# A two-layer graph attention kernel: the order of the setup, and where the first panel's q takes its operands from

## Chip, core and metric

The kernel runs on one core of one Trainium2 chip. The metric is the device time of one execution in microseconds (us); lower is better. The engines are named as the profile names them: PE (TensorE; PEld is its weight load), DVE (VectorE), ACT (ScalarE), POOL (GpSimd) and SP (SyncE). All matrix work is in float32.

## What is computed

Two graph attention layers over N = 2708 nodes with D = 1024 features, each after a layer norm and relu, each added to its input:

```
# layer 0
h = maximum(layernorm(x), 0)
f = h @ Wf + bf;  g = h @ Wg + bg
e = relu(f @ g.T)
scores = where(adj > 0, e, -9e15)
x = x + softmax(scores, axis=1) @ (h @ W + bW)
# layer 1
h = maximum(layernorm(x), 0);  h2 = h @ W1
e = leaky_relu(h2 @ a1 + (h2 @ a2).T, 0.2)
x = x + relu(softmax(where(adj > 0, e, -9e15), axis=1) @ h2)
```

adj is an int32 matrix of N x N with mostly zeros.

## The kernel before

**Layer 0 without f and g.** The kernel forms M = Wf Wg' once (1024 x 1024), so that the scores of all rows against the panel p of columns are h (M h_p') plus bias terms: `project_q(p)` computes q = M' h' for a panel (called B), `scores(p)` multiplies the transposed rows of h with it. The bias terms are dot products on DVE: u and v (weights with bf and bg), r (rows with v).

**Tiling.** The 2708 rows are 22 tiles, 20 of 128 rows and two of 74; they are treated in 11 pairs q = 0..10, the two short tiles being pair 2. The columns are five panels of 586, 586, 512, 512 and 512. Every large product is one level of Strassen and Winograd: seven products of half size named M1, M5, M6, M7, M3, M2, M4, whose operands are sums and differences of blocks, so both the left and the right sides exist in seven variants.

**Setup.** wg's and wf's row chunks (128 x 1024) are loaded and transposed on PE (`transposed_wg` L367, `transposed_wf` L378; PSUM tiles wT_ps), copied to SBUF by DVE and ACT in turn (`copy`, L156), and multiplied: M is made in 16 half rows of eight 128x512 matmuls (`half_row_of_M`, L389, tile M_ps). The half rows with a = 0..7 and b = 0 come first, then those with b = 1. `left_of_q(k)` forms the sums of M's blocks. All 28 left sides (7 products x 4 blocks of 128x512) are written by POOL to the DRAM tensor md_d (`store_M`, L383).

**Rows.** For each pair: `fetch` loads x in four halves; `norms` does the layer norm (DVE statistics, ACT square root L237, ACT relu L249); `rows` is `pair_h`, which forms four sums of halves with `add` and `sub` on DVE into g1 and g2 and writes five pieces to hg_d on POOL (L262 to L264; the right sides of the aggregation later); `dots` gives r; `transposes` transposes the four halves on PE (L299, tile h_ps) and copies them out on ACT (L300, hsT); `sums` forms the four remaining left sides of the scores and writes eight blocks of 128x512 to hs_d[q] on POOL (L312, L313; short pair L316, L317). hsT is a pair of large tiles from a pool (`both`, gts) with a single buffer each; project_q's transposed rows hT are allocated from the same two.

**The order.** These steps stand in a list `later`, each with a cost in us. Between products the program calls `behind(us)`, which adds credit and issues list items until it is used up; `make_until(q)` issues whatever is left up to a pair. The list of before is: for pairs 0 to 3 (EARLY) everything; for pairs 4 to 8 (AHEAD 5) norms, rows, dots; then, for each pair from 4 on, transposes and sums, and norms to dots of the pair five later. Credit is given from half row a = 4 on, 6.5 us per half row. An item that takes PSUM banks is issued only where banks are free, which `scores(0)` gives through make_until(q + 2).

**project_q(0).** It loads the panel's transposed rows (ten loads of hT from hs_d, lo and hi, L121 through `load`), forms T1 (tile qT1) from them, and for each of the seven products loads the left sides (two loads of md from md_d, 0.5 MB each into stream tiles). The products are issued in `accumulate` (L444; PSUM tiles qx, qy, qz) in the order M1, M2, M5, M6, M3, M7, M4; x, y and z are groups of four banks. Evictions go to ACT (M1, M2: m1, B) and DVE (the others).

**scores(p).** For each pair q: make_until(q + 2), the adjacency load of pair q + 2, and products (L877; PSUM sx, sy, sz) in the order M1, M6, M5, M2, M7, M3, M4. Every second product loads its two left sides from hs_d into a stream tile As. M4 of a pair is issued after M1 of the next. The mask of pair q + 1 is converted on DVE after M5, and its transposes on PE with ACT's copies and POOL's write to mk_d (`turn`, L574 to L581) come before M3.

**Queues and buffers.** All loads (`load`, L121) are issued by SP in program order; a load that waits for its buffer holds the loads behind it. The tile framework places instructions and semaphores; in scores of layer 0 the order on DVE is held as written. There are 54 slots (2.3 KB per partition), 12 stream tiles (4 KB per partition) and 8 PSUM banks. g1, g2, md and As are stream tiles; x halves, M and masks are slots.

Of the kernel before, what the change touches and what calls it, by code (L numbers as in the profile page):

```python
# [18 lines left out]
P = 128  # L19
# [37 lines left out]
def kernel(  # L57
# [103 lines left out]
    def put(us, go, fetch=None, takes_psum=False):  # L161
        later.append([us, fetch, go, takes_psum])

    def one():
        for it in later[:2]:
            if it[1]:
                it[1]()
                it[1] = None
        us, _, go, _ = later.pop(0)
        go()  # L170
        return us

    def behind(us, psum_free=False):
        credit[0] = min(credit[0] + us, 2 * us)
        while later and credit[0] > 0 and (psum_free or not later[0][3]):
            credit[0] -= one()
# [5 lines left out]
    def row_to_all(v, name):  # L182
        t = stream(name)
        load(t, bass.AP(tensor=v.tensor, offset=v.offset, ap=[[0, P], [1, D]]))
        return t
# [65 lines left out]
    def pair_h(l, q, ha, hb):  # L251

        n = rows_of[q]
        g1, g2 = stream("g1", (P, 2, W)), stream("g2", (P, 2, W))
        s1, s2, s3, s4 = g1[:n, 0], g1[:n, 1], g2[:n, 0], g2[:n, 1]
        add(s1, ha[1], hb[1])
        sub(s2, s1, ha[0])
        sub(s3, ha[0], ha[1])
        sub(s4, hb[0], s2)
        i, j = group_of[q]  # L260
        for m, h in ((M1, ha[0]), (M2, hb[0]), (M4, hb[1])):
            nc.gpsimd.dma_start(hg_d[l][i][:n, m, j], h)  # L262
        nc.gpsimd.dma_start(hg_d[l][i][:n, M5:M6 + 1, j], g1[:n])
        nc.gpsimd.dma_start(hg_d[l][i][:n, M7:M3 + 1, j], g2[:n])  # L264
# [6 lines left out]
    EARLY, AHEAD = 4, 5  # L271
    made = [0]

    def make_pairs():
        xs, hT = {}, {}

        def fetch(q):
            xs[q] = []
            for t in pairs[q]:
                r0, n = tiles[t]  # L280
                xs[q].append(row_halves("x", n))
                for e in range(2):
                    load(xs[q][-1][e], x[r0:r0 + n, e * W:(e + 1) * W])

        def norms(q):
            for k in range(2):
                normalize(xs[q][k])

        def rows(q):
            pair_h(0, q, *xs[q])  # L290

        def transposes(q):
            n = rows_of[q]
            lo, hi = (t[:, :4 * W].rearrange("p (m c j) -> p m c j", m=4, j=P) for t in both("hsT"))
            hT[q] = lo, hi
            for k, e, o in ((0, 0, lo[:, 0]), (0, 1, lo[:, 3]), (1, 0, hi[:, 3]), (1, 1, hi[:, 2])):
                ps = bank("h_ps", (P, NH, P))
                for c in range(NH):
                    nc.tensor.transpose(ps[:, c, :n], xs[q][k][e][:, c * P:(c + 1) * P], ident[:n, :n])  # L299
                nc.scalar.copy(o[:, :, :n], ps[:, :, :n])  # L300

        def sums(q):
            n = rows_of[q]
            lo, hi = hT.pop(q)
            i = lambda t, k: t[:, k, :, :n]
            add(i(lo, 2), i(hi, 3), i(hi, 2))
            sub(i(lo, 1), i(lo, 2), i(lo, 0))
            sub(i(hi, 0), i(lo, 0), i(hi, 3))
            sub(i(hi, 1), i(lo, 3), i(lo, 1))
            if n == P:  # L310
                flat = lambda t: t.rearrange("p m c j -> p (m c j)")
                nc.gpsimd.dma_start(flat(hs_d[q][:, 0:4]), flat(lo))  # L312
                nc.gpsimd.dma_start(flat(hs_d[q][:, 4:8]), flat(hi))  # L313
            else:
                rows = lambda t: t[:, :, :, :n].rearrange("p m c j -> p (m c) j")
                nc.gpsimd.dma_start(rows(hs_d[q][:, 0:4]), rows(lo))  # L316
                nc.gpsimd.dma_start(rows(hs_d[q][:, 4:8]), rows(hi))  # L317

        def dots(q):
            n = rows_of[q]  # L320
            for k, t in enumerate(pairs[q]):
                dot(r_[:n, t:t + 1], xs[q][k], [vb[e][:n, :W] for e in range(2)], c0[:n])

        def last(q):
            sums(q)
            xs.pop(q)
            made[0] = q + 1

        def start(q):
            put(4.2, lambda: norms(q), lambda: fetch(q))  # L330
            put(2.7, lambda: rows(q))
            put(3.2, lambda: dots(q))

        def end(q):
            put(0.5, lambda: transposes(q), takes_psum=True)
            put(2.7, lambda: last(q))

        for q in range(EARLY):
            start(q)
            end(q)  # L340
        for q in range(EARLY, EARLY + AHEAD):
            start(q)
        for q in range(EARLY, NQ):
            end(q)
            if q + AHEAD < NQ:
                start(q + AHEAD)
# [11 lines left out]
    bfb, bgb = row_to_all(bf, "bfb"), row_to_all(bg, "bgb")  # L358
    wgT, wfT, M = [None, None], {}, {}

    def transposed_wg(b):
        ws = [load_rows(wg, 4 * b + i, "wg") for i in range(4)]
        wgT[b] = [slot(f"wgT{c}_{b}")[:, :W] for c in range(NC)]
        for c in range(NC):
            ps = bank("wT_ps")
            for i in range(4):
                nc.tensor.transpose(ps[:, i * P:(i + 1) * P], ws[i][:, c * P:(c + 1) * P], ident)  # L367
            copy(wgT[b][c], ps)
        for i in range(4):
            dot(u[:, 4 * b + i:4 * b + i + 1], halves(ws[i]), halves(bfb))  # L370

    def transposed_wf(a):
        wt = load_rows(wf, a, "wf")
        wfT[a] = [slot(f"wfT{a}_{e}", (P, NH, P)) for e in range(2)]
        for e in range(2):
            ps = bank("wT_ps", (P, NH, P))
            for c in range(NH):
                nc.tensor.transpose(ps[:, c, :], wt[:, e * W + c * P:e * W + (c + 1) * P], ident)  # L378
            copy(wfT[a][e], ps)
        dot(v[:, a:a + 1], halves(wt), halves(bgb))  # L380

    def store_M(m, k, s):
        nc.gpsimd.dma_start(md_d[:, m, k, :], s)  # L383

    def half_row_of_M(a, b):

        ps = bank("M_ps")
        for c in range(NC):
            nc.tensor.matmul(ps, wfT[a][c // NH][:, c % NH, :], wgT[b][c], start=(c == 0), stop=(c == NC - 1))  # L389
        M[a, b] = slot(f"M{a}_{b}")[:, :W]  # L390
        copy(M[a, b], ps)
        if b == 0:
            store_M(M1 if a < NH else M2, a % NH, M[a, b])

    def left_of_q(k):
        a11, a12, a21, a22 = M.pop((k, 0)), M.pop((k + NH, 0)), M.pop((k, 1)), M.pop((k + NH, 1))
        s1, s2, s4 = (slot(f"ms{i}")[:, :W] for i in range(3))
        add(s1, a21, a22)
        store_M(M5, k, s1)
        sub(s2, s1, a11)  # L400
        store_M(M6, k, s2)
        sub(s4, a12, s2)
        store_M(M3, k, s4)
        sub(a21, a11, a21)
        store_M(M7, k, a21)
        store_M(M4, k, a22)

    make_pairs()
    transposed_wg(0)
    ahead = [0, 1, 2, 3, 4, 5, 6, 7]  # L410
    for a in range(NC):
        for _ in range(2):
            if ahead:
                transposed_wf(ahead.pop(0))
        half_row_of_M(a, 0)
        if a == NH:
            dot(c0, halves(bfb), halves(bgb))
            vb = [slot(f"vb{g}") for g in range(2)]
            for g in range(2):
                spread(vb[g][:, :W], [v[:, 4 * g + j:4 * g + j + 1] for j in range(4)])  # L420
            transposed_wg(1)
        if a >= NH:
            behind(6.5, True)
    for k in range(NH):
        for a in (k, k + NH):
            half_row_of_M(a, 1)
            wfT.pop(a)
            behind(6.5, True)
# [34 lines left out]
    def project_q(p, then={}):  # L463
# [3 lines left out]
        R = both("hT")  # L467
        lo, hi = (t.rearrange("p (c i) -> p c i", c=NH) for t in R)
        o = 0
        for t, (_, n) in enumerate(panels[p], first[p]):  # L470
            q, k = pair_of[t]
# [20 lines left out]
        def left(m, k, d):  # L492
            if m not in L:
                L[m] = [stream(f"md{m}", (P, 2, W)) for _ in range(2)]
                for g in range(2):
                    load(L[m][g], md_d[:, m, 2 * g:2 * g + 2, :])
            return L[m][k // 2][:, k % 2, d * P:(d + 1) * P]
# [8 lines left out]
        def sides(m):  # L506
            for g in range(2):
# [6 lines left out]
                else:  # L514
# [12 lines left out]
                   rate=2.0 if p == 0 else 1.5)  # L527
# [272 lines left out]
    wab = [consts.tile([P, D], FP, name=f"wab{k}") for k in range(2)]  # L800
# [6 lines left out]
    def prepare_W():  # L807
        ab, rows = [], {}

        def fetch(l, k):  # L810
            if l == 1 and not ab:
                for k2, a in enumerate((a1, a2)):
                    load(wab[k2], bass.AP(tensor=a.tensor, offset=a.offset, ap=[[0, P], [1, D]]))
# [37 lines left out]
    def scores(p, B):  # L851
# [50 lines left out]
        for q in range(NQ):  # L902
# [27 lines left out]
            if q + 1 < NQ:  # L930
                turn(q + 1)
            product(q, M3, Y, False)
            add(sa[:n, hi], Y[:n, :h], t[:n, lo])
            finish(q, sa, 0)
            behind(2 * rate, True)
# [5 lines left out]
    def softmax(p, S, m):  # L941
# [20 lines left out]
        later[:0] = [[1.4, None, (lambda i=i: go(i)), False] for i in range(len(order) + LAG)]  # L962
# [125 lines left out]
    def weights1(p, z, m):  # L1088
# [25 lines left out]
        for i in range(len(order) + LAG):  # L1114
            mk = []
            front.append([2.1, (lambda i=i, mk=mk: mk.append(load_mask(p, *order[i]))) if i < len(order) else None,
                          (lambda i=i, mk=mk: go(i, mk)), False])
# [65 lines left out]
```

## Time and profile before

| | |
|---|---|
| median of 3 runs | 3252.6 us (3251.47 to 3255.28) |
| profiled execution | 3251.27 us |
| its span | 3249.5 us |
| mean granted PE clock | 0.986 |
| first matmul of a half row of M | 17.34 us from the start |
| last half row of M ends | 143.4 us |
| first qx product (project_q(0)) | 158.78 us |
| first sx product (scores(0)) | 221.63 us |
| scores(0) ends | 412.94 us |

The page lists per engine the busy time, its share of the span and the number of instructions; then the same in 40 slices of equal length, each digit being tenths (9 is 90% or more), with the clock that TensorE was granted. A line of waits names the engine, what it wanted to do and its line, and after the arrow the engine or transfer and the tile that it waited for, with the total in us, the number of times and the longest. A timeline line has the start and the length in us, then the engine, line, operation, output tile, input tiles, number of instructions, and in brackets the idle time before it. "issue" is waiting that the profile could not put down to an event.

### The profile page before, as it was taken

The numbers are of one execution on the slowest core, as the hardware profiler recorded it, in microseconds if no ns is written. First come the engines' busy times: TensorE is split into PE (matmuls) and PEld (weight loads), VectorE is DVE, ScalarE is ACT, GpSimd is POOL, SyncE is SP. The second block draws the span as 40 slices with busy tenths as digits, with TensorE's granted clock in tenths as the row PEclk, the third lists the DMA queues.
The fourth block names the chain that finished last, engine by engine and source line by source line (L and its number), as shares of the span: only waits on it lengthen the run. The fifth ranks groups of instructions, "written<-read, shape, count | busy, mean of one in ns | idle before, by whom it ended". The sixth has DMA issues, their size and how long they took to land.

```text
span 3249.5 us, 35289 instructions
## 1 busy us (share of the span) xinstructions
PE 3136.1 (97%) x12924; PEld 2330.0 (72%) x12924; DVE 1753.1 (54%) x3648; ACT 499.9 (15%) x833; POOL 326.2 (10%) x410
## 2 busy tenths in 40 slices
PE   8898999999999999999999999996999999999999
PEld 5376777757877578885888885873766748778585
DVE  6856586275732676417672368637665282553712
ACT  2321120010200101101020002103221030221300
POOL 1411001210002110011000101021010000000001
PEclk9999999999999999999999999997999999999999
DMA  5987848565545576457654565765555445555646
GB/s 222 366 276 269 288 160 301 178 225 184 179 131 158 171 249 208 147 184 228 220 181 153 162 200 194 236 236 201 187 166 172 149 154 175 183 191 175 197 149 213
DMA packets 284012, 651.17 MB, mean 200 GB/s; under 512 B 51742, under 2 KB 121362, under 8 KB 281280
## 3 DMA queue, kind: packets, MB, share of 16 engines
q1 hardware_dynamic: 252480, 535.31, 51.1%
q0 software_dynamic: 31360, 113.62, 9.3%
q8 instruction: 102, 1.67, 0.2%
q14 instruction: 70, 0.57, 0.1%
HBM read 535.23 MB, written 113.58 MB: 200 GB/s over the span
## 4 chain that ended last, share of the span: by engine, by line
PE 77%; issue 6%; DVE 4%; DMA 3%; POOL 1%; ACT 1%; POOLq 0%; SPq 0%; DVEq 0%; ACTq 0%
PE gz L444 12%; PE gy L444 12%; PE gx L444 12%; PE sz L877 7%; PE sy L877 5%; PE gv L444 5%; PE sx L877 5%; PE pz L780 4%; PE py L780 3%; PE px L780 3%; PE qz L444 3%; PE qy L444 2%; PE qx L444 2%; DMA hs_d<-hsT 1%; PE mk_ps L574 1%
## 5 line engine op out<-in xcount | busy, mean ns | idle before, releaser
L877 PE MATMUL sz<-B,As 128*128 128x256 f32 (+3 forms) x1320 | 327.5, 397 | 2.9 <-DVE st L44 2.9
L877 PEld LDWEIGHTS sz<-B,As 128*128 128x128 f32 (+1 forms) x1320 | 247.6, 188 | 62.3 <-DVE st L44 3.8
L877 PE MATMUL sx<-B,As 128*128 128x256 f32 (+3 forms) x880 | 224.2, 398 | 13.0 <-DMA As<-hs_d 9.5
L877 PE MATMUL sy<-B,As 128*128 128x256 f32 (+3 forms) x880 | 222.3, 395 | 0.0
L444 PE MATMUL gx<-P,hc 128*128 128x256 f32 (+3 forms) x880 | 204.9, 395 | 4.7 <-ACT P L1107 4.7
L444 PE MATMUL gy<-T,hc 128*128 128x256 f32 (+3 forms) x880 | 205.8, 395 | 3.7 <-DMA hc<-hg_d 2.8
L444 PE MATMUL gz<-Sa,hc 128*128 128x256 f32 (+3 forms) x880 | 206.6, 393 | 0.0
L444 PE MATMUL gz<-P,hc 128*128 128x256 f32 (+3 forms) x880 | 206.3, 393 | 0.0
L877 PEld LDWEIGHTS sx<-B,As 128*128 128x128 f32 (+1 forms) x880 | 164.6, 188 | 53.2 <-issue 9.9
L715 POOL TENSOR_TENSOR gT<-gT,rr 128x2048 f32<-128x2048 f32 (+3 forms) x20 | 68.3, 3433 | 1324.8 <-DVE rr L44 704.2
L444 PEld LDWEIGHTS gx<-P,hc 128*128 128x128 f32 (+1 forms) x880 | 168.6, 192 | 41.1 <-ACT P L1107 5.0
L444 PEld LDWEIGHTS gy<-T,hc 128*128 128x128 f32 (+1 forms) x880 | 168.6, 192 | 39.5 <-DVE wT L44 3.3
L444 PEld LDWEIGHTS gz<-Sa,hc 128*128 128x128 f32 (+1 forms) x880 | 165.5, 190 | 31.9
L444 PEld LDWEIGHTS gz<-P,hc 128*128 128x128 f32 (+1 forms) x880 | 165.5, 190 | 31.9
L877 PEld LDWEIGHTS sy<-B,As 128*128 128x128 f32 (+1 forms) x880 | 160.7, 187 | 34.9 <-issue 0.7
L780 PE MATMUL px<-w,gT 128*128 128x512 f32 x320 | 145.1, 606 | 11.9 <-issue 10.4
L780 PE MATMUL py<-w,ps 128*128 128x512 f32 (+1 forms) x352 | 155.6, 592 | 0.3 <-DVE mcol L44 0.3
L780 PE MATMUL pz<-w,ps 128*128 128x512 f32 (+1 forms) x352 | 155.0, 592 | 0.0
L575 ACT COPY mask<-mk_ps 128x1024 bf16<-128x1024 bf16 (+1 forms) x55 | 55.7, 1013 | 563.8 <-PE mk_ps L574 263.0
L780 PEld LDWEIGHTS pz<-w,ps 128*128 128x128 f32 (+1 forms) x352 | 65.4, 186 | 85.6 <-issue 82.5
L780 PEld LDWEIGHTS py<-w,ps 128*128 128x128 f32 (+1 forms) x352 | 65.4, 186 | 85.6 <-issue 82.5
L780 PEld LDWEIGHTS px<-w,gT 128*128 128x128 f32 x320 | 61.7, 194 | 88.2 <-issue 84.0
(232 smaller groups left out, 4723.9 us busy)
## 6 DMA issues: line engine op xcount, KB each, us to landing
hc<-hg_d SPq DMA_DIRECT2D x350, 512.0 KB
As<-hs_d SPq DMA_DIRECT2D x150, 512.0 KB
w<-wt_d SPq DMA_DIRECT2D x96, 512.0 KB
w<-in_L_gnn_W_dram SPq DMA_DIRECT2D x72, 512.0 KB
md<-md_d SPq DMA_DIRECT2D x70, 512.0 KB
adj_i<-in_adj_dram SPq DMA_DIRECT2D x50, 512.0 KB
hg_d<-g POOLq DMA_DIRECT2D x40, 512.0 KB, 6.1
hs_d<-hsT POOLq DMA_DIRECT2D x20, 1024.0 KB, 8.2
```

What stands on the lines that cost most here:

```text
L444: nc.tensor.matmul(ps[d], left(m, k, d), right(m, k), start=(start and k == 0), stop=(k == K - 1), skip_group_check=True)
L574: nc.tensor.transpose(ps[:n, k, i * P:(i + 1) * P], m[0][:, i, k, :n], identb)
L575: nc.scalar.copy(mk[:n, :, :k4 * P], ps[:n, :, :k4 * P])
L715: nc.gpsimd.tensor_tensor(of(e, s), of(e, s), by(s, k), OP.mult)
L780: nc.tensor.matmul(ps, left[i][m][:, k, :], w_[k], start=(start and k == 0), stop=(k == NH - 1), skip_group_check=True)
L877: nc.tensor.matmul(ps[:n, :h], lefts[q][:, i % 2, c, :n], B[m][c // 2][:, c % 2, :h], start=(start and c == 0), stop=(c == NH - 1), skip_g ...
```

## The change

- wg's four chunks are loaded first, bf and bg after them and among wf's chunks; the two broadcasts live in their own tiles (wab, used later for a1 and a2).
- The first wg block is transposed chunk by chunk into eight banks; wf's, the second wg block's and M's copies out of PSUM are all on ACT; the dots of wg with bf are spread, one per half row.
- The list of due steps is reordered: norms(q + 1), rows(q), transposes(q), dots(q), sums(q), all pairs alike; credit is given from the first half row on (2.0, from a = 4 on 5.0, in the second half 5.5).
- pair_h's four sums are on POOL in layer 0 and stay on DVE in layer 1.
- hsT is four stream tiles, written to hs_d by four DMAs. Where a tile of the pair belongs to panel 0, DVE copies the transposed rows from PSUM also into first_h, the two hT tiles of project_q(0).
- The left sides stay in SBUF slots (m_left) and project_q(0) takes them there; md_d is still written for the other panels.
- project_q(0) gives 1.2 us of credit per product part in place of 2.0; in scores, in all panels, the mask's transposes come after M3 and finish.

```diff
     def pair_h(l, q, ha, hb):
+        on = nc.vector if l else nc.gpsimd
...
-        add(s1, ha[1], hb[1])
-        sub(s2, s1, ha[0])
-        sub(s3, ha[0], ha[1])
-        sub(s4, hb[0], s2)
+        on.tensor_tensor(s1, ha[1], hb[1], OP.add)
+        on.tensor_tensor(s2, s1, ha[0], OP.subtract)
+        on.tensor_tensor(s3, ha[0], ha[1], OP.subtract)
+        on.tensor_tensor(s4, hb[0], s2, OP.subtract)
...
         def transposes(q):
-            lo, hi = (t[:, :4 * W].rearrange("p (m c j) -> p m c j", m=4, j=P) for t in both("hsT"))
+            ts = [stream("hsT", (P, 2, NH, P)) for _ in range(4)]
...
-                nc.scalar.copy(o[:, :, :n], ps[:, :, :n])
+                nc.scalar.copy(hT[q][1](i), ps[:, :, :n])
+                t = pairs[q][k]
+                if panel_of[t] == 0:
+                    o = tiles[t][0]
+                    nc.vector.tensor_copy(first_h[e].rearrange("p (c i) -> p c i", c=NH)[:, :, o:o + n], ps[:, :, :n])
...
-        for q in range(EARLY):
-            start(q)
-            end(q)
-        for q in range(EARLY, EARLY + AHEAD):
-            start(q)
-        for q in range(EARLY, NQ):
-            end(q)
-            if q + AHEAD < NQ:
-                start(q + AHEAD)
+        put_norms = lambda q: put(4.2, lambda: norms(q), lambda: fetch(q))
+        put_rows = lambda q: put(0.5, lambda: rows(q))
+        put_dots = lambda q: put(3.2, lambda: bias(q), ready=lambda: vb[0] is not None)
+        put_norms(0)
+        for q in range(NQ):
+            if q + 1 < NQ:
+                put_norms(q + 1)
+            put_rows(q)
+            put(0.5, lambda q=q: transposes(q), takes_psum=True)
+            if q > 1:
+                put_dots(q)
+            put(2.7, lambda q=q: last(q))
+            if q == 1:
+                put_dots(0)
+                put_dots(1)
...
-    def store_M(m, k, s):
+    def side_of_q(m, k, s):
+        m_left[m, k] = s
         nc.gpsimd.dma_start(md_d[:, m, k, :], s)
...
+    first_h = both("hT")
     make_pairs()
-    transposed_wg(0)
+    ws = fetch_wg(0)
+    rows_of_wf = {0: load_rows(wf, 0, "wf")}
+    bgb = row_to_all(bg, wab[1])
+    rows_of_wf[1] = load_rows(wf, 1, "wf")
+    later[0][1]()
+    later[0][1] = None
+    bfb = row_to_all(bf, wab[0])
+    transposed_wg(0, ws)
...
-        if a >= NH:
-            behind(6.5, True)
+        behind(2.0 if a < NH else 5.0, True)
     for k in range(NH):
         for a in (k, k + NH):
             half_row_of_M(a, 1)
             wfT.pop(a)
-            behind(6.5, True)
+            behind(5.5, True)
         left_of_q(k)
...
     def project_q(p, then={}):
-        R = both("hT")
+        R = first_h if p == 0 else both("hT")
...
         def left(m, k, d):
             if m not in L:
-                L[m] = [stream(f"md{m}", (P, 2, W)) for _ in range(2)]
-                for g in range(2):
-                    load(L[m][g], md_d[:, m, 2 * g:2 * g + 2, :])
-            return L[m][k // 2][:, k % 2, d * P:(d + 1) * P]
+                L.clear()
+                if p == 0:
+                    L[m] = [m_left.pop((m, k)) for k in range(NH)]
+                else:
+                    two = [stream(f"md{m}", (P, 2, W)) for _ in range(2)]
+                    for g in range(2):
+                        load(two[g], md_d[:, m, 2 * g:2 * g + 2, :])
+                    L[m] = [two[k // 2][:, k % 2] for k in range(NH)]
+            return L[m][k][:, d * P:(d + 1) * P]
...
-                   rate=2.0 if p == 0 else 1.5)
+                   rate=1.2 if p == 0 else 1.5)
...
-            if q + 1 < NQ:
-                turn(q + 1)
             product(q, M3, Y, False)
             add(sa[:n, hi], Y[:n, :h], t[:n, lo])
             finish(q, sa, 0)
+            if q + 1 < NQ:
+                turn(q + 1)
             behind(2 * rate, True)
```

## Prediction

> **What bounds the kernel now.** I read the page from the top, then TensorE's order in time, then who waited for what in the stretches that the change touches.
>
> ```profile
> span 3249.5 us, 35289 instructions
> ...
> PE 3136.1 (97%) x12924; PEld 2330.0 (72%) x12924; DVE 1753.1 (54%) x3648; ACT 499.9 (15%) x833; POOL 326.2 (10%) x410
> ...
> PE   8898999999999999999999999996999999999999
> ```
>
> The profiled execution took 3251.27 us: this span and 1.8 us around it. The median of the runs shown is 3252.6, 1.3 more; I sum against 3251.3 and add the 1.3 at the end. TensorE is the bound. The span less its busy time is 113 us, and the edits can only recover idle or slowed TensorE time, since the order of the kernel's instructions beside them shows no less matrix work: transposes and products are the same in number. A slice is 81 us; slices 1, 2 and 4 are below 9, and these are the ones the change touches. From slice 6 (406 us) on, the order of the instructions stays as it is but for the mask transposes. So I took windows over the first 420 us (columns: each engine's busy time, the granted TensorE clock, DMA share, GB/s).
>
> ```profile
> 20.00:140.00 120.00, 120.00 (x396) 61.71 (x395) 93.53 (x243) 39.83 (x71) 34.35 (x59) 1.00 0.74 268
> 140.00:160.00 20.00, 4.60 (x11) 2.08 (x10) 15.87 (x37) 4.11 (x7) 7.64 (x13) 0.71 1.06 391
> 160.00:180.00 20.00, 17.65 (x59) 12.17 (x58) 10.45 (x27) 6.48 (x13) 3.09 (x5) 0.86 1.01 361
> 180.00:220.00 40.00, 40.00 (x171) 30.62 (x170) 23.78 (x53) 5.22 (x9) 3.65 (x6) 1.00 0.72 249
> ...
> 260.00:280.00 20.00, 14.36 (x63) 9.55 (x62) 9.40 (x23) 3.25 (x6) 1.64 (x3) 0.83 0.81 293
> 280.00:300.00 20.00, 17.41 (x80) 13.14 (x79) 16.93 (x39) 6.79 (x12) 3.81 (x7) 0.91 0.62 212
> ```
>
> M's stage has no hole. At 140 to 180 TensorE is nearly empty while the DMA engines are full: that is panel 0's transposed rows and M's left sides being read back. TensorE's timeline there:
>
> ```profile
> 158.78 10.00 PE L444 MATMUL qx<-hT,md 128*128 128x293 f32 x32 [15.40 <-issue]
> 171.14 10.06 PE L444 MATMUL qx<-hT,md 128*128 128x293 f32 x32 [2.35 <-issue]
> ```
>
> "issue" hides the reason; SyncE's timeline names it:
>
> ```profile
> 127.08 18.13 SPq L121 DMA_DIRECT2D hT<-hs_d  x10
> 145.25 2.74 SPq L121 DMA_DIRECT2D md<-md_d  x2
> ```
>
> The ten reads of the rows are issued until 145.2 and the first left sides until 148.0; both must land. In scores of panel 0 (221.63 to 412.94) TensorE's waits are:
>
> ```profile
> PE sx L877 <- DMA As<-hs_d: 8.2, 2, 5.6
> PE sz L877 <- DVE st L44: 2.9, 1, 2.9
> PE h_ps L299 <- DVE Sa L44: 2.4, 1, 2.4
> ```
>
> That is 13.5 us. Products of 8 matmuls behind such holes take 4.25, 3.34 or 3.11 us instead of 2.14; over 2.14 (or 4.12 for 16) the groups lose 2.1, 1.0, 1.2, 0.6, 1.0 and 0.1, so 6.0 us go to the clock. Scores of panel 0 without both are 191.3 - 19.5 = 171.8 us.
>
> **The change, part by part.**
>
> *Start.* M's first half row begins at 17.34. The two bias broadcasts (1.05 MB) leave the head of the load queue; at 391 GB/s that is 2.7 us. One of them and wf's second chunk are still awaited, because their dot products stand ahead of VectorE's wgT copies: seven loads of 0.52 MB instead of six, at 391 GB/s 1.4 us later than the old sixth (9.56, the last wg), so 10.9; the dot 1.5; then up to four copies of 0.62 each, which the eight matmuls (0.43 each) follow. The first half row would start between 13.3 (all of this overlapped) and 17.3 (none gained); I take 14.3, near the low end, as copies and matmuls overlap: **-3.0** (-4 to 0).
>
> *Rows earlier.* Six pairs instead of four are transposed inside M's stage: two more by 1.75 (16 transposes) is +3.5 before project_q, and -3.5 in scores: **0** net, if rows arrive in time. VectorE is 93.53 busy of 120 there and loses the pair adds; DMA is at 0.74 and gets two more pairs of some 4.75 MB, about 0.9 by my estimate. TensorE waits nowhere there by my order. M's stage ends about 143.9 instead of 143.4.
>
> *Rows of panel 0 copied from PSUM, left sides kept.* Ten reads (2.2 MB) and fourteen (7 MB) vanish. Added: ten VectorE copies at 0.69 = 6.9 us, eight of them beside M's products. The first product needs only kept tiles, so the 15.40 goes, and the 2.35 (its second product waited for the next left sides): **-17.75**. Both qx products then run at the usual pace, 7.94 (in the undisturbed stretch after 181 groups of 8 of these matmuls start 1.98 apart, and 32 make 7.94): 10.00 + 10.06 - 15.88 = **-4.2**. What is late next: T1's subtraction, which waits behind pair 7's statistics and the last left side sums on VectorE (I reckon 151.5 against a need at 152.3), and ScalarE's m1 copies behind the square root and relu (151.6 against 152.3). I charge **+0.5** (0 to 2).
>
> The page "TensorE: Matmul & The Clock Gate" of the Trainium skill, section "What's actually happening", says that the clock halves after an idle window of about 3.4 us and is back after 3.4 us of work. The second product, 10.06 after an idle of only 2.35, does not fit that; by the page the clock term would be 1.7 and the total 2.5 later, an estimate.
>
> *pair_h's 44 adds on GpSimd.* VectorE is relieved of 44 x 0.69 = 30 us, which nothing waits for in M's stage. Layer 0 shows no such add on GpSimd; the nearest row is layer 1's, same shape:
>
> ```profile
> L1038 POOL TENSOR_TENSOR x_res<-x_res,bwb x44: 1251/1262/2397, 617.5 to 2162.5; 128x512 f32<-128x512 f32 x40, 74x512 f32<-74x512 f32 x4
> ```
>
> So four adds are 5.04 us (up to 9.6 by the row's maximum). GpSimd's queue is in order: before the adds stands the mask write mk_d, which waits for ScalarE's mask copies (1.01 + 0.29), which wait for the mask transposes. These now come after the M3 product. Behind the adds stand the hg_d writes of g1 and g2 (0.71 each, landing 5.3 later), and the As tile of a coming pair reuses the buffer of g1 or g2; SyncE's load of it waits for that landing and holds all loads behind it. For q = 3 in scores of panel 0: mask copy at 231.7, mk_d 232.8, adds to 237.9, write 238.6, landed 244, As landed 247 to 252, needed 244.7: a hole of 2.5 to 7. The same meeting comes at q = 6, 7 and 8 (pairs 8, 9, 10), reckoned alike: 2 to 6, 0 to 5, 2.5 to 7.5. In exchange the old holes go: x loads for pairs 8 and 9 no longer stand in front of As on SyncE (the 6.85 us issue of four x loads at 256.30 preceded the As loads that TensorE lacked at 272.25). I take 3.5 a meeting, 14, and 3 of slow clock, against 19.5: **-2.5**. Ends: -19.5 (the chain keeps ahead) and +17 (adds of 2.4 lengthen each meeting by 4.6: 14 + 18.4 + 4 of clock = 36.4 against 19.5).
>
> The page "SBUF — State Buffer", section "SBUF: two separate sides", speaks against this part: GpSimd and a VectorE operation with two SBUF inputs lock each other out for whole instructions. By it each add could wait one VectorE add of 0.69, some 11 us more over the four chains, an estimate; the row's median 1262 beside minimum 1251 shows no such wait, its maximum 2397 may.
>
> *Two fewer pair transposes in scores of panel 0*, already counted: -3.5 there, +3.5 in M. *Mask transposes later, in all panels:* they only move on TensorE; the four later scores have 4.8 us of As waits together (the page's 13.0 before sx, 9.5 of it As, less the 8.2 above), so there is little to gain, and a mask is needed only an iteration later: -3 to +3, I take 0. *Smaller writes of hs_d* (four of 0.5 MB for two of 1 MB): two more issues of 0.55 per pair on GpSimd, beside work, and ScalarE's 50.2 us of waiting for the landing of the former pair's write vanish because the tiles come from the stream pool: part of why pairs can be early, no term of its own.
>
> **Sum:** -3.0 - 17.75 - 4.2 + 0.5 - 2.5 = -27; 3251.3 - 27 = 3224.3, and on the median's footing 3225.6. Ends of the unknown adds: 17 better, 3209, or 19.4 worse, 3245.
>
> **Rivals.**
> *Chain keeps ahead.* Buffers come free earlier than my order says and scores run without holes: -19.5 instead of -2.5 there, about 3209. For it: GpSimd is 10% busy. Against: the in-order queue, not the share, makes the wait.
> *Chain bites deeper.* Adds at 1.9, between median and maximum, make each meeting 2.6 longer: 14 + 10 + 6 of clock = 30 instead of 17, 13 worse: about 3239. For it: VectorE is 54% busy and works on the same tiles' rows beside the adds.
> *The gap only moves.* q's start waits for the rows of a pair that came late through the 0.9 full DMA, or 28 kept tiles keep the x loads waiting: 15 of the 17.75 come back: about 3241; with the deeper chain 3254, no change. Against: the order shows no load that q's first product waits for. That the change does not do what it says lies here too.
> *Slower.* GpSimd becomes the pace of pair making in scores of panel 0. A pair costs it 5.0 to 9.6 of adds, 3.1 of hg_d issues (3 x 0.55, 2 x 0.71), 2.2 of hs_d issues, and up to two landings of 6 that its queue stands still for: 10.3 to 27 us. The price is what a pair takes beyond one iteration (7 products and a mask, about 15 us): at 27, 12 for each of five pairs, 60 less the 30 regained before them (27 and the 2.5 of the other reckoning): about 3281. It decides from 6 us beyond an iteration, a pair of 21. Against: five pairs have eleven iterations, and the landings overlap the other pair's work.
>
> **Chances.** Forecast (3219 to 3233) 0.49; chain ahead (3203 to 3219) 0.20; deeper or half moved (3233 to 3246) 0.20; no change 0.06; slower 0.05. About 0.2%, 6.5 us, is what a measurement of this kernel can tell from none; so faster 0.89, same 0.06, slower 0.05. The range 3207 to 3246 takes in the ends of the adds (3209 and 3245) with 1 to 2 us of the start's and q's; it leaves out no change, slower and the last of the chain ahead, under 0.15.
>
> **What would show it.** First M_ps matmul at 14.3; qx about 144 with no idle before it and clock 1.00 in 140 to 180; first sx about 200.6; pair_h's adds on GpSimd at 1.26 (the changed kernel's L258 to L261); holes before sx put down to As, with GpSimd's g writes just ahead. Wrong if qx still waits, or if scores of panel 0 take over 200 us, or if anything after them moves by more than 3.

## The result, and the profile after

The changed kernel takes 3236.0 us (median of 4 runs, 3233.5 to 3237.2) against 3253.9 for the kernel before beside it: ratio 0.9943, 95% interval 0.9926 to 0.996. That is 17.9 us faster; I forecast 27. The range (3207 to 3246) holds the time, but it lies outside the stretch that I took for the likeliest (3219 to 3233, chance 0.49), in that of a deeper chain or a half moved gap (3233 to 3246, 0.20). The profiled execution took 3237.2, the slowest of the four, while that of before, 3251.3, was among the fastest, so the two profiles differ by only 14.

The page of the changed kernel, its span, its busy time and its TensorE row by slices:

```profile
span 3235.3 us, 35363 instructions
...
PE 3137.1 (97%) x12924; PEld 2333.4 (72%) x12924; DVE 1756.3 (54%) x3594; ACT 507.7 (16%) x853; POOL 395.0 (12%) x476
...
PE   8999999999999999999999998997999999999998
```

TensorE's busy time is the same within 1 us (3136.1 before); what went is idle time. Slices 2 and 4 are 9 now. TensorE's timeline of the changed kernel at the start and around q (start, length, line and operation, idle before it in brackets):

```profile
4.49 5.89 PE L377 MATMUL wT_ps<-ident,wg 128*128 128x128 f32 x32 [4.49 <-DMA wg<-in_L_gnn_Wg_dram]
...
15.26 2.39 PE L401 MATMUL wT_ps<-ident,wf 128*128 128x128 f32 x12 [4.06 <-DVE wgT L44]
17.44 7.90 PE L413 MATMUL M_ps<-wgT,wfT 128*128 128x512 f32 x16
...
147.75 8.06 PE L478 MATMUL qx<-hT,M 128*128 128x293 f32 x32
155.65 0.66 PE L478 MATMUL qy<-qT,ms 128*128 128x293 f32 x2
156.14 8.06 PE L478 MATMUL qx<-hT,M 128*128 128x293 f32 x32
```

The first transposes start 3.8 us earlier, but a new idle of 4.06 eats all of it: M's first half row is at 17.44, where it was at 17.34. q follows M's stage without a hole, and both qx products take 8.06 where they took 10.00 and 10.06. Stage by stage, from the timelines of the profiled executions (us):

| stage | before | after | forecast difference | difference |
|---|---|---|---|---|
| first half row of M starts | 17.3 | 17.4 | -3.0 | +0.1 |
| M's stage | 126.1 | 130.5 | +3.5 | +4.4 |
| end of M to first scores product | 78.2 | 56.2 | -21.5 | -22.0 |
| scores of panel 0 | 191.3 | 185.9 | -6.0 | -5.4 |
| all after that | 2836.6 | 2845.2 | 0 | +8.6 |

The start and the last row are where the forecast of 27 was too high. The holes that remain in scores of panel 0, from TensorE's timeline of the changed kernel, and what SyncE's queue waited for between 220 and 345 us (total, times, longest):

```profile
250.48 2.21 PE L917 MATMUL sx<-B,As 128*128 128x293 f32 x8 [0.83 <-DMA As<-hs_d]
299.81 4.25 PE L917 MATMUL sx<-B,As 128*128 128x293 f32 x8 [4.05 <-DMA As<-hs_d]
333.11 0.97 PE L615 MATMUL mk_ps<-identb,nm 128*128 128x128 bf16 x8 [2.28 <-DVE nm L44]
343.77 3.74 PE L917 MATMUL sx<-B,As 128*128 128x293 f32 x8 [4.27 <-DMA As<-hs_d]
```

```profile
SPq L121 <- DMA hg_d<-g: 45.4, 6, 15.3
SPq L121 <- DMA hs_d<-hsT: 18.6, 3, 12.2
```

Three of these are meetings that the prediction named, at pairs q = 3, 6 and 8, with 0.8, 4.1 and 4.3 us, and the queue that waits for the landing of g is the one it named; at q = 7 there is no such hole. The 2.3 us are something else: there TensorE waits for the mask that VectorE converts (nm). VectorE's and GpSimd's timelines of the changed kernel just before:

```profile
325.88 4.07 DVE L44 SCALAR_TENSOR_TENSOR Sb<-Sb,mask 128x586 f32<-128x586 f32 x1
329.99 1.72 DVE L44 TENSOR_TENSOR acc<-acc,Sb 128x586 f32<-128x586 f32 x1
332.37 0.68 DVE L44 TENSOR_SCALAR nm<-adj_i 128x1024 bf16<-128x1024 int32 x1
```

```profile
325.58 1.28 POOL L259 TENSOR_TENSOR g<-x 128x512 f32<-128x512 f32 x1
...
329.40 1.68 POOL L262 TENSOR_TENSOR g<-x,g 128x512 f32<-128x512 f32 x1
```

The first two of VectorE's take 0.77 us each where no sum runs on GpSimd. Here the first lasts beyond the end of GpSimd's third sum (329.33), so nm is late, and TensorE with it.

### The profile page after: what moved, and what is told of

Its sections match the earlier page's. It is cut to its first block, busy times and chain, and to the rows that moved or that the text cites. A ratio compares the mean times of both kernels' runs of the same rounds, so it can differ in the third digit from the quotient of the medians.

```text
span 3235.3 us, 35363 instructions
## 1 busy us (share of the span) xinstructions
PE 3137.1 (97%) x12924; PEld 2333.4 (72%) x12924; DVE 1756.3 (54%) x3594; ACT 507.7 (16%) x853; POOL 395.0 (12%) x476
## 5 line engine op out<-in xcount | busy, mean ns | idle before, releaser
L917 PEld LDWEIGHTS sx<-B,As 128*128 128x128 f32 (+1 forms) x880 | 162.3, 189 | 51.4 <-issue 11.2
```

The source lines that it names most:

```text
L917: nc.tensor.matmul(ps[:n, :h], lefts[q][:, i % 2, c, :n], B[m][c // 2][:, c % 2, :h], start=(start and c == 0), stop=(c == NH - 1), skip_g ...
```

## The experiments

All ran on a chip beside the kernel before, in five rounds; the ratio with its interval is against that kernel. The first five change one thing each in the changed kernel.

**start.** VectorE's order is held as written until wf's first chunks are transposed.

```diff
+    nc.hold = True
     transposed_wg(0, ws)
     for a in range(NC):
...
             transposed_wf(i)
+        nc.hold = False
         half_row_of_M(a, 0)
```

> The changed kernel, with VectorE's order held as written until wf's first two chunks are transposed: the four wgT copies then stand ahead of the dot products of wf with bg. Theory: the 4.06 us that TensorE waits for wgT, and the late first half row at 17.44, come only from these dots, which wait for bg's broadcast (landed 12.36). Then the copies end by 13.0, the first half row starts between 12.5 and 14.0, everything after is 3.5 to 5 earlier, and the time is 3231 to 3233 against 3236. Rival: the next limit (wf's later chunks behind the x loads, or ScalarE's copies) eats it: first half row under 15, but M's stage ends less than 1.5 earlier and the time is 3235 to 3237.

3231.0 us, 0.9924 (0.9908 to 0.9939). VectorE's timeline in the changed kernel shows the cause: the dot of wf with bg's broadcast (wab) waits 10.79 us for its load and stands before the wgT copies.

```profile
12.36 0.69 DVE L44 SCALAR_TENSOR_TENSOR junk<-wf,wab 128x512 bf16<-128x512 f32 x1 [10.79 <-DMA wab<-in_L_gnn_bg_dram]
...
14.52 2.48 DVE L44 COPY wgT<-wT_ps 128x512 f32<-128x512 f32 x4
```

With the copies first, TensorE waits only for wf's second chunk (TensorE's timeline of this run):

```profile
13.62 1.06 PE L401 MATMUL wT_ps<-ident,wf 128*128 128x128 f32 x8 [1.60 <-DMA wf<-in_L_gnn_Wf_dram]
14.52 7.03 PE L413 MATMUL M_ps<-wgT,wfT 128*128 128x512 f32 x16
```

14.52 instead of 17.44, and M's stage ends at 144.1 instead of 147.9. The theory holds, the half row a little later than expected (12.5 to 14.0). The interval overlaps the changed kernel's; that it is a gain rests on the timeline.

**turn.** The mask transposes go back before M3, in all panels.

```diff
+            if q + 1 < NQ:
+                turn(q + 1)
             product(q, M3, Y, False)
...
             finish(q, sa, 0)
-            if q + 1 < NQ:
-                turn(q + 1)
             behind(2 * rate, True)
```

> The changed kernel with the mask transposes back before M3 in scores of all panels. After scores of panel 0 the changed kernel gives back 8.6 us by its profile (22.8 ahead there, 14.2 at the end), of which 3.9 in scores of panel 2, 2.0 in panel 4 and 2.8 in the first aggregation. Theory: the later masks cause the losses in the scores; then this kernel regains 3 to 6 there, scores of panel 0 lose under 2, and the time is 3230 to 3234. Rival: these are scatter from one execution to another and the place of the transposes does nothing after panel 0: 3235 to 3239, with losses of the same size at other places.

3232.4 us, 0.9929 (0.9914 to 0.9944). Scores of panel 0 take 187.0 (185.9), of panel 2 147.7 (151.5), of panel 4 142.8 (144.8). One profile could be scatter, so I read scores of panel 4 in all fourteen profiles of this study: the six kernels with the later masks there have 144.8, 146.3, 146.2, 145.2, 146.2 and 146.4, the eight with the earlier ones 142.7 or 142.8 (five) and 137.9 (three), so every one of the first is above all of the second. That is shown. In panel 2 the ranges are 146.9 to 151.5 and 147.0 to 147.8, so there the loss is not in every kernel with the later masks. TensorE's waits in scores of panel 4, changed kernel and then this one:

```profile
PE sz L917 <- DVE st L44: 4.9, 1, 4.9
```

```profile
PE sx L917 <- DVE sm L44: 3.1, 1, 3.1
```

Both are waits for VectorE once, near the panel's end, where the eviction comes late. The profiles with 142.7 or 142.8 have the second wait (2.8 to 3.1), those with 137.9 have none there, and all six with the later masks have the first (4.9 to 5.2). The first aggregation, which took 2.8 more in the changed kernel, has 162.1 to 167.6 over the fourteen profiles without regard to any edit: that part is scatter.

**adds.** pair_h's four sums go back to VectorE.

```diff
-        on = nc.vector if l else nc.gpsimd
+        on = nc.vector
```

> The changed kernel with pair_h's four sums on VectorE in layer 0. Theory: SyncE's 45.4 us of waiting for hg_d<-g in scores of panel 0 hang on the 5 us of adds in GpSimd's queue; with the adds on VectorE the g writes come about 5 us earlier, the holes of 0.8, 4.1, 2.3 and 4.3 us shrink to less than half and scores of panel 0 take 179 to 182 instead of 185.9: 3230 to 3233. Rival: VectorE's held order in scores puts the adds behind evictions that wait for TensorE, so the chain stays as long and the evictions behind the adds come 2.8 us later: scores of panel 0 186 to 195, 3236 to 3245.

3225.7 us, 0.9911 (0.9896 to 0.9927), 10.3 less than the changed kernel. Scores of panel 0 take 177.2 instead of 185.9, and TensorE has two holes in place of the four (TensorE's timeline of this run):

```profile
305.58 2.25 PE L917 MATMUL sy<-B,As 128*128 128x293 f32 x8 [0.85 <-DVE st L44]
321.96 4.24 PE L917 MATMUL sy<-B,As 128*128 128x293 f32 x8 [5.92 <-DMA As<-hs_d]
```

GpSimd's timeline in the changed kernel shows what stood in its queue (L259 to L262 are the sums, L266 and L267 the writes of g1 and g2):

```profile
281.58 1.28 POOL L259 TENSOR_TENSOR g<-x 128x512 f32<-128x512 f32 x1
282.81 1.26 POOL L261 TENSOR_TENSOR g<-x 128x512 f32<-128x512 f32 x1
284.04 1.25 POOL L260 TENSOR_TENSOR g<-g,x 128x512 f32<-128x512 f32 x1
285.37 1.70 POOL L262 TENSOR_TENSOR g<-x,g 128x512 f32<-128x512 f32 x1
287.02 0.73 POOL L266 DMA_DIRECT2D hg_d<-g  x1
287.75 0.73 POOL L267 DMA_DIRECT2D hg_d<-g  x1
```

and SyncE's timeline what came of it:

```profile
291.86 2.35 SPq L121 DMA_DIRECT2D As<-hs_d  x4
```

The As loads are issued when g has landed, and TensorE gets its first at 299.81. The 5.5 us of sums are in this chain link by link. With this kernel SyncE waits 29.8 us for hg_d<-g in seven waits (195 to 420 us), where it was 45.4 in six. The chain of the theory is there and the rival, that the sums would hold up VectorE's evictions, is not. But the gain is larger than the theory had it (179 to 182 us for the scores, 3230 to 3233 in all), and the chain is only a part: the holes before As went from 9.2 us to 5.9, those behind VectorE from 2.7 (the 2.3 and one of 0.4) to 0.9, and the rest is clock. With the sums back on VectorE, none of its 20 multiplications with the mask in scores of panel 0 takes more than 0.78 us, in this run and in the seven other kernels that have them there; in each of the six with the sums on GpSimd three or four take 1.6 to 4.1. VectorE's other instructions, up to the end of scores of panel 0, add up to 267.3 us here and to 300.7 in the changed kernel: moving 30 us of sums away lengthened the others by 33. The scheduler also moved one group of pair transposes in this kernel, so the 8.7 us are of the edit and what follows from it in the order, and how much of them is the chain's and how much VectorE's is not shown.

**md.** Left sides read back for project_q(0).

```diff
-                if p == 0:
+                if False:
                     L[m] = [m_left.pop((m, k)) for k in range(NH)]
```

> The changed kernel with the left sides of project_q(0) read back from DRAM (14 loads, 7 MB), all else as changed. Theory: of the 21.9 us gained between the end of M's stage and the first product of scores, the rows and the left sides each account for the first gap while the other is there; the left sides of M1 and M2 are written early, but the last sums of M5 and later only at the end of M's stage, and they must be written (6 to 9 us) and read (6 to 8 us): a wait of 6 to 14 at M5 or M2 and 2 to 4 of clock, 3244 to 3254. Rival: all that matters is the rows; left sides are prefetched into stream tiles behind M's products and cost under 3: 3236 to 3239.

3247.4 us, 0.9978 (0.9968 to 0.9988), 11.4 more, as the theory had it. In q there is one hole, at the second product, and its clock (TensorE's timeline of this run):

```profile
167.51 10.19 PE L478 MATMUL qx<-hT,md 128*128 128x293 f32 x32 [12.19 <-DMA md<-md_d]
```

**rows.** Panel 0's transposed rows read back, left sides kept.

```diff
-        R = first_h if p == 0 else both("hT")
+        R = both("hT")
...
-            if p == 0:
-                break
...
-                t = pairs[q][k]
-                if panel_of[t] == 0:
-                    o = tiles[t][0]
-                    nc.vector.tensor_copy(first_h[e].rearrange("p (c i) -> p c i", c=NH)[:, :, o:o + n], ps[:, :, :n])
```

> The changed kernel with panel 0's transposed rows read back from hs_d (ten loads, 2.2 MB) in place of the copies from PSUM; left sides still kept. Theory 1: the reads cost as much as the left sides did (their second gap, 12.2, and the clock behind it, 2.1): first qx 6 to 16 after M's stage, 3244 to 3254. Theory 2: before, the reads were late because hT shared its two tiles with hsT, whose last write had to land first; hsT are stream tiles now, so the reads are issued during M's stage and hide: q starts within 2 us of M's end, 3234 to 3239, and the copies from PSUM were not needed.

3235.7 us, 0.9942 (0.9928 to 0.9956): nothing. The timeline has 0.82 and 0.94 us of waiting in q, 2.3 in all between M's end and scores (58.5 against 56.2). Theory 2 holds in its number: the ten reads, issued from 128.4 to 152.0, hide. Its reason, that the reads had been late through the tiles shared with hsT, does not: the kernel before issues them from 127.1 on, and keep (below) shares these tiles too and has no gap.

**reads.** Both edits together.

> The changed kernel with both the rows and the left sides of project_q(0) read back; the new order, GpSimd's adds and the loads as changed. If rows cost by themselves (theory 1), this is the old gap again: some 3252 to 3260. If the rows hide (theory 2), this is the run with the left sides alone within 3: 3244 to 3251.

3257.8 us, 1.0012 (1.0003 to 1.0021). The number is in the range of theory 1, but neither theory is right: the rows cost nothing alone and 10.4 us on top of the left sides. TensorE's and SyncE's timelines of this run:

```profile
156.97 10.19 PE L473 MATMUL qx<-hT,md 128*128 128x293 f32 x32 [10.44 <-DMA md<-md_d]
172.55 10.71 PE L473 MATMUL qx<-hT,md 128*128 128x293 f32 x32 [5.39 <-issue]
```

```profile
116.19 24.99 SPq L121 DMA_DIRECT2D hT<-hs_d  x10
141.29 3.85 SPq L121 DMA_DIRECT2D md<-md_d  x2
```

The rows are in front of the left sides in one queue. It is the left sides that TensorE then waits for; in the run with these alone, the first two were issued at 133.73 and the first product began at once. The rest of the change, without what it does for q, is worth nothing: it is even 0.1% slower than the kernel before.

**keep.** So the kernel before got the left sides alone, all else as it was.

```diff
     def store_M(m, k, s):
+        m_left[m, k] = s
         nc.gpsimd.dma_start(md_d[:, m, k, :], s)
...
+                if p == 0:
+                    L[m] = [m_left.pop((m, k)) for k in range(NH)]
```

> The kernel before with one edit: the left sides stay in SBUF and project_q(0) takes them from there; order, rows, loads as before. Theory: the 28 kept tiles are the part that pays. Of the 15.40 ahead of q the ten row reads remain (issued 127.1 to 145.2, landing some 8 later, about 152), so the first gap shrinks to 7 to 11, and the 2.35, its clock and the queueing of md go: 3240 to 3246. Rival 1: hT shares its tiles with hsT in this kernel, so the reads are as late as the whole gap, and only the second goes: 3247 to 3251. Rival 2: 28 of 54 slots held make x loads late, so that scores of panel 0 lose what q gains: 3250 or more.

3226.8 us, 0.9918 (0.9904 to 0.9931): one edit gains 26, by medians more than the whole change, though its interval overlaps that of the changed kernel by 0.0005. I had expected 3240 to 3246. SyncE's and TensorE's timelines of this run:

```profile
127.03 18.17 SPq L121 DMA_DIRECT2D hT<-hs_d  x10
```

```profile
143.29 15.95 PE L445 MATMUL qx<-hT,M 128*128 128x293 f32 x64
159.08 8.07 PE L445 MATMUL qy<-qT,ms 128*128 128x293 f32 x32
```

The ten reads are where they were (127.08 and 18.13 in the kernel before), and q still starts with M's end, with 64 matmuls unbroken at full clock. Without the reads of the left sides the whole 15.40 is gone, not the half of it. From M's end to scores it takes 57.7 us, 20.5 less than before; scores of panel 0 take 192.3, like before. So 20.5 of the 26 are where the edit acts. The two profiles differ by 23.2: scores of panel 4 are 4.8 shorter (137.9 against 142.7) and the first aggregation is 4.5 longer, neither for a reason that these runs show.

**all3** is start, turn and adds together; **all3b** the same with the masks behind M3 in panel 0 only.

> Three edits on the changed kernel together: wgT copies ahead of the bg dots, pair_h's sums on VectorE, mask transposes before M3. Alone they took 5.0, 10.3 and 3.7 us off by medians. Theory: they act at different places (start, scores of panel 0, scores of panels 2 and 4) and add: 3216 to 3221. Rival: VectorE's adds already regained what the masks cost in panel 2 (146.8 there with the sums on VectorE against 151.4), so the masks bring only panel 4's 2 or nothing: 3220 to 3225.

> As the three edits together, but the mask transposes stay behind M3 in panel 0 and go before it in panels 1 to 4 only. Theory: the later place is of use in panel 0 alone (scores of panel 0 took 187.0 with the old place, 185.9 with the new) and costs 2 to 4 in panels 2 and 4: 1 us below the three edits together. Rival: no difference beyond 2 us between the two.

all3: 3221.3 us, 0.9897 (0.988 to 0.9915). all3b: 3221.3, 0.9895 (0.9877 to 0.9912). Together they gain 14.8 us of the 19.0 that they gain one by one. Scores of panel 0 take 179.9 and 178.3, of panel 2 147.1 and 147.8, which fits the rival (146.9 in adds, with the masks still late); panel 4 has 142.7 in both. The place of the masks in panel 0 makes no difference that these runs can tell.

**order.** Rows and left sides read back, and the three edits.

> The changed kernel with rows and left sides read back, and with the three edits (wgT copies first, sums on VectorE, mask transposes before M3): the new order of the setup by itself. Theory: the three edits add as they did with the operands kept (16 to 19), from 3257.8: 3238 to 3243, so the new order has a worth of its own of some 12 in scores of panel 0, which GpSimd's sums had hidden. Rival: with q's gap open pairs have time anyway, the sums' place matters less, and the time is 3246 to 3255.

3237.6 us, 0.9954 (0.9941 to 0.9966). The theory holds, in place and, within 0.4 us, in number: scores of panel 0 take 179.1 instead of the 186.9 of reads. Treating the rows earlier is worth some 12 us in scores (191.3 before), of which 3.5 moved into M's stage, and GpSimd's sums had hidden 8 of them. Scores of panel 4 are at 137.9 here too, 4.8 less than in the profile before.

**all4** is all3 with bg loaded behind wf's second chunk; **all4r** has the rows read back on top of it.

```diff
-    bgb = row_to_all(bg, wab[1])
     rows_of_wf[1] = load_rows(wf, 1, "wf")
+    bgb = row_to_all(bg, wab[1])
```

> The three edits together, and bg's broadcast loaded behind wf's second chunk, since TensorE waited 2.25 us for that chunk there. Theory: first half row of M 1.0 to 1.5 earlier (13.2 to 13.6 from 14.5) and nothing else: 3219 to 3221. Rival: no difference that can be measured, 3221 to 3223, because bg's dots end later and delay the first normalization on VectorE.

> As the run before, but with panel 0's rows read back from hs_d and not copied from PSUM. Theory: with the left sides kept and hsT in the stream pool the reads hide behind M, as in the run with the rows alone (2.6 us in q, nothing by medians): within 3 of the run before. Rival: with M's stage ending 4 earlier the ten reads, issued by 152 in that run, are late by 4 more: 4 to 8 slower than the run before.

all4: 3218.2 us, 0.989 (0.9875 to 0.9905), the best kernel here, M's first half row at 13.05; the gain over all3 is within the intervals. all4r: 3229.3, 0.9924 (0.9909 to 0.9938), 11.1 more: the rival was right in kind, and more than its 4 to 8. TensorE's and SyncE's timelines of all4r:

```profile
151.29 18.38 PE L475 MATMUL qx<-hT,M 128*128 128x293 f32 x64 [8.98 <-DMA hT<-hs_d]
```

```profile
123.10 31.27 SPq L121 DMA_DIRECT2D hT<-hs_d  x10
```

M's stage ends at 142.3, 5.9 earlier than in rows, and the reads are issued until 154.4, 2.4 later: 8.3 of the 8.98. So the copies from PSUM cost or gain nothing while M's stage ends at 148 and are worth 11 when it ends at 142: 8.98 of waiting, and 2.4 of clock in the 64 matmuls (18.38 against keep's 15.95). (Its profiled execution, 3221.7, was the fastest of its five.)

## Why the prediction was right, and where it was not

**What bounds.** Right: only idle or slowed TensorE time was recovered. The sum was 9 us too good, by the start and by what came after scores of panel 0; there my own sign of being wrong, a move of more than 3, came true with 8.6. That the time stayed in the range owes something to luck, as the 8.6 was in no term.

**Start, -3.0.** Wrong: +0.1. I saw that the bg dots stand ahead of the wgT copies and put the wait at 10.9, as if loads landed at 391 GB/s one after the other. bg landed at 12.36, and then a dot and a half (2.2 us) and four copies (2.48) came before wf's transposes could end, as TensorE itself waited for the copies out of PSUM (4.06 <-DVE wgT), which I had not in the sum. start puts the cost of that order at 2.9 us.

**Rows earlier, 0 net.** Right in size: two more pairs are in M's stage, which is 4.4 longer (3.5 of it the pairs, most of the rest the clock of the first two half rows, 7.90 for 16 matmuls against 7.03). No wait there, as reckoned.

**The q part, -17.75 - 4.2 + 0.5 = -21.5.** Right in size (-22.0), but I gave the first gap to the rows and the left sides together. Keeping the left sides alone removes it (keep). Copying the rows alone from PSUM, with the left sides read back (md), leaves a hole of 12.2 at the second product; the first two left sides do not stand behind the rows there and are in time. So the rows' copying is of use only with a shorter M stage (all4r) or where the left sides are read back behind the rows (reads). I also called TensorE nearly empty at 140 to 180; by the row shown that holds to 160 (4.60 of 20 us), and from 160 to 180 it was busy for 17.65, at a clock of 0.86.

**Adds on GpSimd, -2.5 in all.** The net is right in size (-5.4 in scores of panel 0, with the 3.5 of the transposes, against -6.0), the mechanism in part. The chain through GpSimd's queue is shown link by link and cost 9.2 us of holes against 14, with none at q = 7. Another 2.7 came from VectorE's instructions that GpSimd's sums lengthened, which the sum left out, and the clock took some 6 against 3 (an estimate, what is left of 185.9 after the 171.8 without holes, less 3.5, and the holes). That these errors cancel is luck. What I did not ask is what the same kernel gives with the sums left on VectorE: the loss was the cost of the edit, 8.7 us in scores by adds, and not a fate of the new order. The edit does not even shed VectorE time: VectorE is busy for 1756.3 us with the sums on GpSimd and for 1748.7 with them back on VectorE.

**SBUF lock.** The page "SBUF — State Buffer" of the Trainium skill (section "SBUF: two separate sides") has GpSimd and a VectorE instruction with two SBUF inputs lock each other out for whole instructions. The trace agrees, but the wait is on the other side than I reckoned it. GpSimd's sums hardly wait: for 128 rows they have means of 1.29, 1.32, 1.31 and 1.47 us against 1.25 at the least. VectorE's instructions with two SBUF inputs do: the multiplication with the mask takes 3.62, 1.85 and 4.07 us beside the sums and 0.77 elsewhere, while those with one input from PSUM (sm<-sx,rb, 0.46) stay as they are beside the sums. I had looked at GpSimd's durations alone, in the row of layer 1.

**Masks later, 0 (-3 to 3).** Wrong by 2.0 to 3.6 in scores of panel 4 and, in some kernels, up to 4 in panel 2; I had reasoned from a sum of waits that the mask had an iteration of slack, and not looked at the last iterations. That sum was misread besides: the 4.8 us are all of TensorE's idle time before sx in the later scores, and only 1.3 of it (9.5 less 8.2) is As. The remaining 2.8 of the 8.6 lost behind scores of panel 0 were scatter. Why TensorE's one wait near the end of panel 4 is there in five profiles with the earlier place and not in three is open; it was not tried.

**Rivals.** "Deeper" gave 3239, about the time seen, but by adds of 1.9 us, which were 1.25 to 1.79, most of them under 1.3. Something like "the gap only moves" happened at the start, on a smaller scale. "Chain ahead", "no change" and "slower" did not come near.

## What to carry to other kernels

Before a gap with two transfers in front of it is put down to both, take one away: here the gap went when 14 reads of 7 MB that the core had itself written were left out, and the rows in front of them, which cost nothing alone, only made it worse through the shared queue. Moving arithmetic to an engine that also issues DMAs puts it in front of these DMAs, of the buffers that they release and of the loads that wait for those buffers, so it is priced in the chain and not by the engine's share. It can also lengthen what stays behind: look at the durations of both engines while they run side by side. When a large change gains, undo it edit by edit: one of its parts gave 26 us, and the rest, as made, gave 9 of them back by medians (in the profiles scores of panels 2 and 4 are 11.2 longer than in keep, a part of it without a cause that is known).

## What the runs showed that I had not expected

TensorE lost clock after some holes that are shorter than those of the rule that I weighed. In the changed kernel 2.28 us of idle ahead of the mask transposes were followed by 8 matmuls in 3.51 us instead of 2.14, with a granted clock of 0.53 from 333 to 336 us; in start the same 2.28 were followed by 3.35. But in rows 2.30 us and in reads 2.29 us of idle at the same place were followed by 2.22, so no loss, and in keep 1.22 us cost nothing (8.17 for 32 matmuls). The rule of the page "TensorE: Matmul & The Clock Gate" of the Trainium skill (section "What's actually happening", an idle window of about 3.4 us) does not cover the 2.28. What decides whether such a hole costs is not shown.
